# One list of 62 regular edges for each row in place of two lists of 32, in a sparse graph-attention kernel

## The chip, the core and the metric

The kernel runs on one core of one Trainium2 chip. The metric is device time in microseconds (us) for one execution. TensorE is called PE (its weight loads PEld), VectorE DVE, ScalarE ACT, GpSimd POOL, and SyncE SP.

## The reference

There are 3327 nodes with 128 features each, and a dense adjacency matrix in which about 64 entries of a row are not zero. Two layers follow each other: a four-head attention layer, in which only the nonzero entries of the row count, and a normalised graph convolution. Cut to what matters:

```python
def head(x, A, w1, w2, a, Wlin):              # x: layer-normed and relu'd features
    E = leaky_relu((x @ w1)[:, None, :] + (x @ w2)[None, :, :], 0.01)
    s = jnp.tanh(E @ a / 8.0) * 8.0
    s = jnp.exp(s) * A
    s = s / jnp.sum(s, axis=-1, keepdims=True)
    return leaky_relu(s @ x @ Wlin.T, 0.01)

x = x + concatenate([head(h, adj, ...) for 4 heads]) @ w
# layer 1: A_t = adj + I, D its row sums
x = x + relu(D^-1/2 A_t D^-1/2 @ (relu(layernorm(x)) @ W.T + b))
```

## The kernel before

The kernel treats the adjacency as lists of edges. The rows are padded to 3328, which makes 26 blocks of 128 rows, and each block is worked through in two halves of 64 rows (half-blocks, `hb`).

**Lists.** For each row, `prep` codes the columns of the nonzero entries (L401), takes the eight largest codes of each of 64 segments (L405), and draws from the left and the right half of the columns a sorted list of SLOTS = 32 edges each, eight at a time: a MAX8 (L434) gives eight, a MATCH_REPLACE (L436) strikes them out. These 64 edges are the row's regular slots. What is left over goes into up to EXTRA = 40 further entries (L457, L460), and those of 64 rows are packed into three tiles of extra edges (OVT = 3), addressed by the comparison matrix `oi`. If any edge did not fit, a flag would send the whole program down a dense path after the sparse one; this is not seen in the profile.

**Tiles.** A regular tile has 128 edges: 8 rows of the block by 16 slots. A half-block thus has 32 regular tiles in four windows `w` of WT = 8 tiles, and a fifth window (w = NW = 4) with the three extra tiles. The row numbers in tile order come from a product of the lists, spread by `modsel` (L440), with `tmask` (L447, L450: `idx`); `pex` brings each row's score term into tile order in the same way (L541).

**Gathers.** For each tile, POOL issues one indirect DMA (L562), which brings 128 table rows of up to 709 floats: 64 adjacency weights, 133 features and sums, and four heads of 128 projected features. The windows have four buffers `g`, the extra tiles one buffer `ge`.

**Stages.** Half a window, four tiles, is a stage m (m = 0 to 7 regular, m = 8 the extra tiles). `stage_z`: for each head PE transposes the four tiles into z (L587), and DVE takes the maximum with the negative own projection of the row, x1n (L599, into r); in m = 8 PE adds the own projection (L590) and ACT does the relu (L596). `stage_r`: PE reduces r with `sel` to scores s (L610). After each window, `finish` runs: ACT copies the scores (L618), DVE picks the adjacency weights of each edge out of the gathered rows (`wq`, L622, with `qmask`), PE turns the scores (L627), DVE adds two terms (sc, L630 and L633), ACT computes tanh and exp, DVE multiplies exp and weight into `wt` (L649), and PE adds everything up into `ag` with eight products (L658), each with 32 columns of weights: 4 heads by 8 rows. For the extra tiles, the weights `wo` cover all 64 rows (L665, L667), and ag takes six products of 128 columns (L676). `close` then finishes the half-block.

**Order.** The program's order on every engine is fixed when the kernel is built. The loop over stages calls `slot()` six times for each stage. At each slot the running `finish` and `close` generators take one step (up to their next `yield`), `advance` takes a share of the NPREP = 72 steps of the next preparation, and `fetch` issues what gathers have a buffer. At the start of a block the next block's preparation is half done, so that the coding and most list rounds of the next but one fall into the second half-block, and the index products, extra rounds and `oi` into the first. In program order, the finish of window 3 (stages 6 and 7) starts at the end of stage m = 8; its products into `wt` are issued at the start of the next half-block's stage m = 1, and its ag products at that stage's end; the finish of the extra tiles comes one stage later.

```python
            for i in range(-1, n + 1):
                if i + 1 < n:
                    slot()
                if 0 <= i < n:
                    ...
                    rs[i] = stage_z(blks[b], hb, m, slot)
                if 0 <= i - 1 < n:
                    ...
                    stage_r(blks[b], hb, m, rs.pop(i - 1))
                    if m % 2 or m == NG - 1:
                        ends.append(finish(blks[b], hb, m // 2))
                    slot()
```

Of the kernel before, what the change touches and what calls it, by code (L numbers as in the profile page):

```python
# [9 lines left out]
F32 = mybir.dt.float32  # L10
AF = mybir.ActivationFunctionType
OP = mybir.AluOpType
AX = mybir.AxisListType
# [46 lines left out]
SLOTS = 32  # L60
EXTRA = 40
# [3 lines left out]
COLS = 709  # L65
FEAT = 64
# [162 lines left out]
def _sparse_layers(tc, nc, x, adj, w1, w2, a, wlin, w, gw, gb, gb_sb, gwT, x_sb, dinv, flag, ident, out):  # L229
# [18 lines left out]
    NT = 32  # L248
    NG = 9
    WT = 8  # L250
    NW = NT // WT
    LATE = 1

    with ExitStack() as l0:
# [16 lines left out]
        tmask = res.tile([P, 16], F32, name="tmask")  # L271
        modsel = res.tile([P, P], F32, name="modsel")
        qmask = res.tile([P, 8], F32, name="qmask")
        hoff = res.tile([P, 2], F32, name="hoff")
        lower = res.tile([P, P], F32, name="lower")
        first = res.tile([P, 16], F32, name="first")
# [19 lines left out]
        nc.gpsimd.iota(first, [[0, 2], [16, 4], [0, 2]], base=0, channel_multiplier=0, allow_small_or_imprecise_dtypes=True)  # L296
# [7 lines left out]
        for down in (hoff, rowid):  # L304
            nc.vector.tensor_scalar(down, down, -1.0, float(NP), op0=OP.mult, op1=OP.add)

        nc.gpsimd.affine_select(tmask, ones[:, :16], [[-8, 16]], OP.is_ge, 0.0, base=0, channel_multiplier=1)
        nc.gpsimd.affine_select(tmask, tmask, [[8, 16]], OP.is_ge, 0.0, base=7, channel_multiplier=-1)

        nc.gpsimd.affine_select(qmask, ones[:, :8], [[-16, 8]], OP.is_ge, 0.0, base=0, channel_multiplier=1)  # L310
        nc.gpsimd.affine_select(qmask, qmask, [[16, 8]], OP.is_ge, 0.0, base=15, channel_multiplier=-1)
# [32 lines left out]
        def prep(b, k):  # L344
# [21 lines left out]
            def known_step(j0, js, at):  # L366
# [5 lines left out]
                if j0 == 0:  # L372
                    k.part1 = pb.tile([P, P], F32, name="part1")
                    nc.scalar.copy(k.part1, pq[:, :P])
                else:
                    nc.vector.tensor_add(k.part1, k.part1, pq[:, :P])
# [52 lines left out]
            lists = pb.tile([P, 64 + 46], F32, name="lists")  # L429
            k.lists = lists  # L430
            for c in range(2):
                for r in range(SLOTS // 8):
                    top = lists[:, SLOTS * c + 8 * r:SLOTS * c + 8 * r + 8]
                    nc.vector.max(top, cand[:, c, :SOME])  # L434
                    yield
                    nc.vector.match_replace(out=cand[:, c, :SOME], in_to_replace=top, in_values=cand[:, c, :SOME], imm_value=0.0)  # L436
                    yield

            lq = pb.tile([P, 4, 8, 16], F32, name="lq", bufs=1)
            nc.vector.tensor_tensor(lq, modsel.rearrange("p (q s) -> p q s", q=8)[:, None].to_broadcast([P, 4, 8, 16]),  # L440
                                    lists[:, :64].rearrange("p (c s) -> p c s", c=4)[:, :, None, :].to_broadcast([P, 4, 8, 16]), OP.mult)
            yield
# [3 lines left out]
            for c in range(4):  # L446
                nc.tensor.matmul(pm[:, 16 * c:16 * c + 16], lq[:, c].rearrange("p q s -> p (q s)"), tmask, start=True, stop=True)  # L447
            yield
            idx = pb.tile([P, NW, 16], mybir.dt.int32, name="idx")
            nc.vector.scalar_tensor_tensor(idx, pm[:, :64].rearrange("p (c t) -> p c t", c=4), -float(ROW),  # L450
                                           first[:, None, :].to_broadcast([P, NW, 16]), op0=OP.mult, op1=OP.add)
            k.idx = idx
            yield
            flat = cand[:, :, :SOME]
            for r in range(EXTRA // 8):
                top = lists[:, 64 + 8 * r:64 + 8 * r + 8]
                nc.vector.max(top, flat)  # L457
                yield
                if r < EXTRA // 8 - 1:
                    nc.vector.match_replace(out=flat, in_to_replace=top, in_values=flat, imm_value=0.0)  # L460
                yield
# [7 lines left out]
            ext = lists[:, 64:]  # L469
            some = pb.tile([P, EXTRA], F32, name="some")  # L470
            cnt = pb.tile([P, 1], F32, name="cnt")
            nc.vector.tensor_scalar(some, ext[:, :EXTRA], 0.0, None, op0=OP.is_gt, op1=OP.add, accum_out=cnt)
            nc.scalar.copy(ext[:, 41:42], rowid)
            nc.scalar.copy(ext[:, 42:42 + H], p_all[:, b, H:])
# [5 lines left out]
            nc.vector.tensor_sub(ext[:, 40:41], hoff[:, :1], pm[:, :1])  # L480
            end = pb.tile([P, 1], F32, name="end")
            nc.vector.tensor_sub(end, ext[:, 40:41], cnt)
# [3 lines left out]
            nc.vector.tensor_reduce(lsum, lists[:, :64 + EXTRA], AX.X, OP.add)  # L486
# [8 lines left out]
            nc.vector.tensor_scalar(oi, code[:, :2 * OVT * P], ext[:, 40:41], None, op0=OP.is_le)  # L495
# [7 lines left out]
            ex_ps = pm[:, :2 * OVT * 46].rearrange("p (t c) -> p t c", c=46)  # L503
# [3 lines left out]
            ex = pb.tile([P, 2 * OVT, 46], F32, name="ex")  # L507
# [3 lines left out]
            nc.vector.tensor_sub(rel, epos, ex[:, :, 40])  # L511
# [19 lines left out]
            for h in range(H):  # L531
# [3 lines left out]
            pmx = pb.tile([P, 16, H], F32, name="pmx")  # L535
            nc.vector.tensor_tensor(pmx, tmask[:, :, None].to_broadcast([P, 16, H]),
                                    p_all[:, b, None, :H].to_broadcast([P, 16, H]), OP.mult)
# [9 lines left out]
        def rows_in():  # L547
            state["turn"] += 1
            return pgs[state["turn"] % 4].tile([P, WT, ROW], F32, name="g")
# [246 lines left out]
        def allow(kind):  # L796
            state[kind] += 1
# [509 lines left out]
```

## Time and profile before

| | before |
|---|---|
| median of three runs | 2530.59 us (2528.16 to 2538.27) |
| the profiled execution | 2536.74 us, span 2534.9 us |
| busy share: PE, DVE, POOL, ACT | 90%, 80%, 71%, 28% |
| DMA | 838.58 MB, mean 331 GB/s |
| gathers | 1664 regular and 156 extra, mean 971 and 978 ns on POOL |
| first gather, first z, last regular gather | 67.1, 76.0, 2422.6 us |

The span is the time from the first instruction to the last in one profiled execution. A line of a group gives the source line, engine, operation, what is written and read, shapes and count; then the busy time in us, the mean of one instruction in ns, and the idle time of the engine just before these instructions with what ended it. Busy time counts overlapping instructions once, so it can be less than count times mean. A line of the timeline gives start, duration and, in brackets, the idle time before it. A line of the waits gives the total, the number and the longest of the waits of one line for another. PE's ends are modelled, so a busy PE is not PE at its peak.

### The profile page before, as it was taken

Reading aid. Unit: us, or ns where it says so; the run is one execution under the profiler, and the core shown is the slowest. Engines: PE = TensorE matmul, PEld = TensorE weight load, DVE = VectorE, ACT = ScalarE, POOL = GpSimd, SP = SyncE. Lnnn points to the kernel's source line nnn. Section 1 sums busy time; section 2 is a strip of 40 time slices with the busy share of each in tenths; the row PEclk is TensorE's granted clock in tenths of the full one; section 3 lists DMA queues with packets and bytes.
Section 4 is the critical chain, followed back from the end, with each engine's and each line's share of the span. In section 5 each row is a group of like instructions: output and inputs, shape, how many; then the busy total and the mean of one; then the engine's idle time right before and its main releaser. Section 6 shows DMA issues by size and latency. Waiting matters only on the chain.

```text
span 2534.9 us, 51974 instructions
## 1 busy us (share of the span) xinstructions
PE 2278.9 (90%) x19410; PEld 1586.2 (63%) x19410; DVE 2030.5 (80%) x6260; ACT 704.1 (28%) x1651; POOL 1791.8 (71%) x1873
## 2 busy tenths in 40 slices
PE   6689899988989998989998999999999899999898
PEld 4456666656666666666666666666666667675553
DVE  7678988888788888878888788988988888895433
ACT  4122233223223222322322322232232233222110
POOL 3577777777777777777777777777777777777620
PEclk9789999999999999999999999999999999999999
DMA  9999999999999999999999999999999999999995
GB/s 294 392 338 314 342 353 318 334 351 335 324 339 346 318 328 359 329 319 343 337 312 336 353 311 341 352 329 329 339 346 318 330 360 313 333 322 347 324 336 186
DMA packets 460759, 838.58 MB, mean 331 GB/s; under 512 B 209099, under 2 KB 318165, under 8 KB 457173
## 3 DMA queue, kind: packets, MB, share of 16 engines
q0 software_dynamic: 145600, 640.34, 71.0%
q1 hardware_dynamic: 219396, 140.96, 19.1%
q10 hardware_dynamic: 95504, 53.88, 7.0%
q8 instruction: 156, 2.56, 0.4%
q14 instruction: 103, 0.84, 0.1%
HBM read 765.93 MB, written 113.42 MB: 347 GB/s over the span
## 4 chain that ended last, share of the span: by engine, by line
PE 35%; DVE 24%; DMA 20%; POOL 11%; issue 7%; ACT 1%; SPq 0%; DVEq 0%; POOLq 0%; ACTq 0%
DMA g<-table,idx 13%; DVE r L599 11%; POOL g L562 10%; PE z L587 10%; PE s L610 6%; PE z L590 3%; DMA ge<-table,idxo 3%; PE z L937 2%; DVE cand L405 2%; PE tr L627 2%; PE ag L658 2%; DMA AT_d<-at 2%; PE tr L370 2%; PE tr L505 1%; DVE codes L401 1%
## 5 line engine op out<-in xcount | busy, mean ns | idle before, releaser
L562 POOL DMA_INDIRECT g<-table,idx x1664 | 1616.3, 971 | 568.3 <-issue 442.2
L599 DVE TENSOR_TENSOR r<-z,x1n 128x1024 f32<-128x1024 f32 x832 | 1010.1, 1215 | 65.5 <-PE z L587 63.9
L587 PE MATMUL z<-ident,g 128*128 128x128 f32 x6656 | 922.4, 278 | 151.9 <-DVE r L599 111.7
L587 PEld LDWEIGHTS z<-ident,g 128*128 128x128 f32 x6656 | 743.8, 142 | 366.9 <-DVE r L599 224.2
L610 PE MATMUL s<-r,sel 128*32 128x512 f32 (+1 forms) x3744 | 491.1, 597 | 0.7 <-ACT ssb L618 0.7
L618 ACT COPY ssb<-s 128x512 f32<-128x512 f32 x260 | 146.7, 564 | 524.6 <-PE s L610 522.5
L630 DVE TENSOR_TENSOR sc<-tr,g 128x32 f32<-128x32 f32 x208 | 38.5, 185 | 300.5 <-PE tr L627 300.5
L405 DVE MAX8 cand<-codes 128x8 f32<-128x52 uint16 x1664 | 215.3, 205 | 0.0
L562 POOL DMA_INDIRECT ge<-table,idxo x156 | 152.6, 978 | 47.5 <-issue 38.1
L638 ACT ACTIVATE th<-sc 128x32 f32<-128x32 f32 x260 | 58.3, 224 | 420.9 <-DVE sc L633 418.5
L590 PE MATMUL z<-oi,x1b 128*128 128x384 f32 x416 | 174.1, 501 | 0.0
L658 PEld LDWEIGHTS ag<-g,wt 128*32 128x32 f32 x3328 | 99.0, 110 | 115.3 <-issue 100.8
L357 ACT COPY at<-tr 128x512 f32<-128x512 f32 (+1 forms) x175 | 97.0, 554 | 222.2 <-PE tr L355 198.3
L627 PE MATMUL tr<-ident,ssb 128*128 128x128 f32 x988 | 153.1, 276 | 5.0 <-ACT ssb L618 4.5
L610 PEld LDWEIGHTS s<-r,sel 128*32 128x32 f32 x3744 | 73.9, 108 | 110.5 <-issue 86.4
L587 PEld LDWEIGHTS z<-ident,ge 128*128 128x128 f32 x624 | 81.4, 146 | 94.8 <-issue 28.5
L596 ACT ACTIVATE r<-z 128x768 f32<-128x768 f32 x104 | 84.3, 810 | 201.7 <-PE z L590 201.7
L658 PE MATMUL ag<-g,wt 128*32 128x133 f32 x3328 | 133.4, 278 | 0.0
L587 PE MATMUL z<-ident,ge 128*128 128x128 f32 x624 | 111.7, 283 | 21.1 <-DMA ge<-table,idxo 18.5
L627 PEld LDWEIGHTS tr<-ident,ssb 128*128 128x128 f32 x988 | 114.3, 141 | 15.3 <-ACT ssb L618 14.9
L355 PE MATMUL tr<-ident,adjb 128*128 128x128 f32 x676 | 107.4, 282 | 16.3 <-DMA adjb<-in_adj_dram 10.2
L401 DVE SCALAR_TENSOR_TENSOR codes<-adjb,code 128x832 uint16<-128x832 f32 x104 | 102.3, 1020 | 1.9 <-DMA adjb<-in_adj_dram 1.9
(188 smaller groups left out, 2350.4 us busy)
## 6 DMA issues: line engine op xcount, KB each, us to landing
adjb<-in_adj_dram SPq DMA_DIRECT2D x26, 1664.0 KB
table<-AT_d SPq DMA_DIRECT2D x52, 832.0 KB
AT_d<-at ACTq DMA_DIRECT2D x150, 256.0 KB
g<-table,idx POOLq DMA_INDIRECT x1664
table<-img SPq DMA_DIRECT2D x12, 1312.0 KB
adjb<-AT_d SPq DMA_DIRECT2D x18, 512.0 KB
g<-AT_d SPq DMA_DIRECT2D x7, 1024.0 KB
g<-AT_d ACTq DMA_DIRECT2D x5, 1024.0 KB
```

Of the source, the lines that this page charges most:

```text
L355: nc.tensor.transpose(pt[:, q, :], adjb[:, (j0 + q) * P:(j0 + q + 1) * P], ident)
L357: nc.scalar.copy(at[:, :n, :], pt[:, :n, :])
L401: nc.vector.scalar_tensor_tensor(codes[:, i], adjb[:, c0:c0 + part], 0.0, code[:, c0:c0 + part], op0=OP.not_equal, op1=OP.mult, accum_out= ...
L405: nc.vector.max(cand[:, c, 8:].rearrange("p (r s) -> p r s", s=32)[:, :, sgm % 32], codes.rearrange("p a b -> p (a b)")[:, sgm % 32 * SEG: ...
L562: return nc.gpsimd.indirect_dma_start(out=g[:, t, lo:COLS], out_offset=None, in_=tab, in_offset=bass.IndirectOffsetOnAxis(ap=at[:, t:t + 1 ...
L587: nc.tensor.matmul(z[:, i, q * P:(q + 1) * P], g[:, m % 2 * 4 + q, PROJ + h * D:PROJ + (h + 1) * D], ident, is_transpose=True, start=(q == ...
L590: nc.tensor.matmul(z[:, i, :n], k.x1b[:, h * D:(h + 1) * D], k.oi[:, hb * n:(hb + 1) * n], start=False, stop=True, skip_group_check=True)
L599: nc.vector.tensor_tensor(r.rearrange("p h (i s) -> p h i s", s=16), z.rearrange("p h (i s) -> p h i s", s=16), k.x1n[:, 2 * hp:2 * hp + 2 ...
L610: nc.tensor.matmul(k.s[32 * h:32 * h + 32, :n], sel[:, h, 31 - at:63 - at], rs[h // 2][:, h % 2, :n], start=(at == 0), stop=(at == 1 or m ...
L618: nc.scalar.copy(ssb[:, :nk * P], s[:, :nk * P])
L627: nc.tensor.transpose(pt[:, q, :], ssb[:, q * P:(q + 1) * P], ident)
L658: nc.tensor.matmul(ag[32 * cg:32 * cg + 32, u, :WORK], wt[:, t].rearrange("p h q -> p (h q)"), g[:, t, FEAT:FEAT + WORK], start=(w == 0 an ...
```

## The change

Each row now has one list of 62 regular edges, taken over all columns: two rounds of eight from either half, then further rounds over both halves together, which run on into the EXTRA = 42 entries of extra edges. The first 48 slots make three windows of eight tiles as before (8 rows by 16 slots). The last 14 slots make seven tiles in three shapes: four of 16 rows by 8 slots, two of 32 rows by 4 slots, one of 64 rows by 2 slots. The fourth window thus has LAST = 7 tiles, and a half-block 31 regular tiles and three of extra edges. Masks, index products, `pex`, r, `wq`, sc and the ag products follow the shapes; the last window's weights are written into `wo`, and its `wq` into the buffer of `am`, both shared with the extra tiles. A gathered row takes 712 places of its buffer in place of 720. NLIST and NPREP grow by two. `part1`, `pmx` and `some` have one buffer instead of two.

The core of the diff:

```diff
-SLOTS = 32
-EXTRA = 40
+SLOTS = 62
+EXTRA = 42
+WIDE = 712
...
+    LAST = WT - 1
+    SHAPE = ((8, 0, 16), (16, 16, 8), (32, 24, 4), (64, 28, 2))
+    EX = EXTRA + 6
...
-            for c in range(2):
-                for r in range(SLOTS // 8):
-                    top = lists[:, SLOTS * c + 8 * r:SLOTS * c + 8 * r + 8]
-                    nc.vector.max(top, cand[:, c, :SOME])
-                    yield
-                    nc.vector.match_replace(out=cand[:, c, :SOME], in_to_replace=top, in_values=cand[:, c, :SOME], imm_value=0.0)
-                    yield
+            both = cand[:, :, :SOME]
+            parts = [cand[:, c, :SOME] for c in range(2) for _ in range(2)] + [both] * ((SLOTS + EXTRA) // 8 - 4)
+            def lists_step(r):
+                top = lists[:, 8 * r:8 * r + 8]
+                nc.vector.max(top, parts[r])
+                yield
+                if r < len(parts) - 1:
+                    nc.vector.match_replace(out=parts[r], in_to_replace=top, in_values=parts[r], imm_value=0.0)
+                yield
+            for r in range(8):
+                yield from lists_step(r)
+            def by_tile(at, n, i):
+                rows = SHAPE[i][0]
+                slots = P // rows
+                big = [P, n, rows, slots]
+                nc.vector.tensor_tensor(lq[:, max(0, i - 1):max(0, i - 1) + n]..., OP.mult)
+            lq = pb.tile([P, 3, P], F32, name="lq", bufs=1)
+            by_tile(0, 3, 0)
...
+            lq = pb.tile([P, 3, P], F32, name="lq", bufs=1)
+            for i, at in ((1, 48), (2, 56), (3, 60)):
+                by_tile(at, 1, i)
...
+            for i, to in enumerate((pm[:, :16 * H], last[:, :, :4 * H], last[:, :, 4 * H:6 * H], last[:, :, 6 * H:])):
+                _, at, n = SHAPE[i]
+                nc.tensor.matmul(to, modsel[:, i], pmx[:, at:at + n].rearrange("p t h -> p (t h)"), start=True, stop=True)
...
         def stage_z(k, hb, m, slot):
-            n = 4 * P if m < 8 else OVT * P
+            n = 4 * P if m < LAST else OVT * P
...
+                    half = HALF * hb
+                    for lo, hi, slots, r0 in (((0, 2 * P, 4, half), (2 * P, 3 * P, 2, half)) if m == LAST else ((0, 4 * P, 8, half),)
+                                              if m == LAST - 1 else ((0, 4 * P, 16, half + 32 * (m % 2)),)):
+                        u = (hi - lo) // slots
+                        nc.vector.tensor_tensor(r[:, :, lo:hi]..., z[:, :, lo:hi]..., k.x1n[...], OP.max)
...
         def finish(k, hb, w):
+            if w == NW - 1:
+                wq = pb.tile([P, OVT, HALF], F32, name="am", bufs=1)
+                for i, (t, n) in enumerate(((0, 4), (4, 2), (6, 1))):
+                    ...
+                    nc.vector.tensor_tensor(wq[:, i]..., diag, qmask[...], OP.mult)
...
+            for at, m, n in ((0, 2, 4),) if nt == WT else ((0, 1, 4), (4, 1, 3)) if nt == LAST else ((0, 1, OVT),):
+                nc.vector.tensor_tensor(sc[:, at:at + m * n]..., pt..., g[...]..., OP.add)
...
+            if w == NW - 1:
+                wo = pv.tile([P, OVT, 8, H, 8], F32, name="wo")
+                for i, (t, n) in enumerate(((0, 4), (4, 2), (6, 1))):
+                    u = 8 // n
+                    for c in range(n):
+                        nc.vector.tensor_tensor(wo[:, i, u * c:u * c + u], pe[:, t + c, None, :, None].to_broadcast([P, u, H, 8]),
+                                                wq[:, i]..., OP.mult)
+                ...
+                for i, (t, n) in enumerate(((0, 4), (4, 2), (6, 1))):
+                    u = min(4, 8 // n)
+                    for c in range(8 // u):
+                        o = 32 * (u * c % 4)
+                        nc.tensor.matmul(ag[o:o + 32 * u, u * c // 4, :WORK], wo[:, i, u * c:u * c + u].rearrange("p g h q -> p (g h q)"),
+                                         g[:, t + (c if n > 1 else 0), FEAT:FEAT + WORK], start=False, stop=False, skip_group_check=True)
+                allow("g")
+                return
...
-        NLIST = 42
-        NPREP = 72
+        NLIST = 44
+        NPREP = 74
```

## The prediction

> **What bounds the kernel now.** I read the page first, for the engines and the costliest groups.
>
> ```profile
> PE 2278.9 (90%) x19410; PEld 1586.2 (63%) x19410; DVE 2030.5 (80%) x6260; ACT 704.1 (28%) x1651; POOL 1791.8 (71%) x1873
> L562 POOL DMA_INDIRECT g<-table,idx x1664 | 1616.3, 971 | 568.3 <-issue 442.2
> L599 DVE TENSOR_TENSOR r<-z,x1n 128x1024 f32<-128x1024 f32 x832 | 1010.1, 1215 | 65.5 <-PE z L587 63.9
> ```
>
> The 71% of POOL is deceptive: between gathers of 0.95 us lies an issue gap of 0.30 us (442.2 us in 1442 gaps), so a gather holds POOL for 1.25 us, and the 35 gathers of a half-block (64 rows) for 43.8 us. The queue is nearly full. So the next view is the time of one half-block: I take the first transpose into z (L587) of each half-block from the timeline and cut the windows there, four in a row.
>
> ```profile
> 1628.63:1672.89 44.26, 41.20 (x374) 29.41 (x370) 35.68 (x94) 11.49 (x33) 33.59 (x36) 1.00 0.99 317
> 1672.89:1716.73 43.84, 40.85 (x375) 29.43 (x371) 40.64 (x142) 14.83 (x31) 33.22 (x35) 1.00 1.00 354
> 1716.73:1760.99 44.26, 41.20 (x374) 29.41 (x371) 35.68 (x94) 11.49 (x33) 33.60 (x36) 1.00 0.97 311
> 1760.99:1805.48 44.49, 41.76 (x384) 30.38 (x380) 40.91 (x143) 14.71 (x31) 33.83 (x35) 1.00 1.00 358
> ```
>
> Columns: window, length, busy us of PE, PEld, DVE, ACT, POOL, clock, DMA share, GB/s. A first half-block (the first and third row) takes 44.26 us each time, with the same busy times to 0.01; of the 24 first half-blocks between 195 and 2298 us, 19 lie within 0.2 us of that. Data that arrived late would not repeat so. A second half-block takes 43.05 to 44.7 when nothing disturbs it. Next, who waits for whom between 200 and 2300 us:
>
> ```profile
> DVE sc L630 <- PE tr L627: 250.4, 80, 8.3
> PEld z L587 <- DVE r L599: 238.7, 239, 2.6
> PE z L587 <- DMA ge<-table,idxo: 17.9, 21, 2.4
> PE z L587 <- DMA g<-table,idx: 5.7, 12, 1.3
> POOL g L562 <- issue: 397.8, 1300, 1.6
> ```
>
> TensorE and VectorE wait for each other, hardly for data. So the half-block's length is a chain through PE and DVE, in fixed order, and the gathers run beside it at almost the same pace: they win only where the extra tile (ge) arrives late. Comparing stage lengths with their undisturbed values, I find such delays in 16 of the 47 half-blocks, 31.9 us in all. That is what fewer gathers can give back.
>
> Where the chain has room is seen in DVE's timeline:
>
> ```profile
> 1678.62 0.42 DVE L649 TENSOR_TENSOR wt<-pe,wq 128x256 f32<-128x256 f32 x1
> 1682.99 0.64 PE L658 MATMUL ag<-g,wt 128*32 128x133 f32 x16
> 1683.33 0.28 DVE L665 SCALAR_TENSOR_TENSOR am<-code,ex,ge 128x64 f32<-128x64 uint16 x1
> 1683.71 0.42 DVE L667 TENSOR_TENSOR wo<-pe,am 128x256 f32<-128x256 f32 x1
> ...
> 1714.75 0.30 DVE L434 MAX8 lists<-cand 128x8 f32<-128x136 f32 x1
> 1717.86 0.19 DVE L630 TENSOR_TENSOR sc<-tr,g 128x32 f32<-128x32 f32 x1 [2.42 <-PE tr L627]
> ```
>
> In the stage of extra tiles (m = 8) DVE idles: 2.42 us here, at the end of a second half-block, and 6.11 us at the end of a first one (1674.02). Elsewhere in a second half-block it is never free (40.6 busy + 2.4 = 43.0 of 43.84), so DVE work added there lengthens it one for one. In a first half-block it has about 2.5 us of other room.
>
> **Two rules of the Trainium skill.** "VectorE: DVE Perf Modes", section on the TRN2 errata, says that an fp32 tensor_tensor takes (N+151)/0.96 ns, a fixed part per instruction, so small pieces are dear. The trace agrees: N = 512 gives 691 (L440 shows 682), N = 256 gives 424 (L649: 416), N = 64 gives 224 (L622: 219). For 128 and 384 elements I interpolate the trace: 283 and 549. Not all of it is engine time: eight MAX8 with a mean of 205 ns take 1.01 us, so 0.08 of each overlaps its neighbour, and I charge duration less 0.08. "TensorEngine Tiling (Array Packing)", section Theoretical Speedup, says that weights of at most 32 columns run up to four at once, of at most 64 two, and wider ones alone. Again the trace agrees, and it has the price:
>
> ```profile
> L658 PE MATMUL ag<-g,wt 128*32 128x133 f32 x3328 | 133.4, 278 | 0.0
> L676 PE MATMUL ag<-ge,wo 128*128 128x133 f32 x624 | 79.4, 277 | 0.0
> L649 DVE TENSOR_TENSOR wt<-pe,wq 128x256 f32<-128x256 f32 x208 | 86.5, 416 | 0.0
> L434 DVE MAX8 lists<-cand 128x8 f32<-128x136 f32 x208 | 61.6, 296 | 1.3
> L436 DVE MATCH_REPLACE8 cand<-lists,cand 128x136 f32<-128x136 f32 x208 | 59.0, 284 | 0.0
> L457 DVE MAX8 lists<-cand 128x8 f32<-128x272 f32 x130 | 57.3, 441 | 2.7
> ```
>
> 133.4/3328 = 0.040 us for each 32-column instruction, 79.4/624 = 0.127 for each of 128 columns.
>
> **The change, part by part.** *Removed:* one of 35 gathers, 52 in all: 52 x 1.25 = 65 us of POOL, and 52 x 0.33 MB = 17 of 839 MB. Both lie beside the chain; worth only the 32 us of late data above. In stage m = 7 PE loses four transposes, and s (L610) in the next stage shrinks from 1.06 to 0.85 us (the 384-column form at 1675.23): -0.21, on the path, since PE is full in the ge stage. r of m = 7 becomes 512 + 256 elements: L914 690 and 425 for L599's 1215, less overlap -0.18, twice: -0.36.
>
> *Added in each finish of w = 3.* Seven multiplications into wo (four of 64, two of 128, one of 256 elements) for one wt: 4 x 0.14 + 2 x 0.20 + 0.345 - 0.335 = +0.97 us of DVE at the start of stage m = 1. One more sc: +0.09. Two more wq: +0.28, queued in the idle of the ge stage; free (0.28 each if that idle were gone). The eight ag matmuls keep their number (sixteen instructions) but become 64 and 128 columns wide: 8 x 0.064 (half of 0.127, as the page has it) + 8 x 0.127 = 1.53 for 0.64: +0.9 of PE. wo has one buffer, shared with the extra tiles' wo of the stage after (L667). So a **new wait**: the first L667 must wait until PE has read the old wo. In a second half-block ag ends at 1683.63 and L667 starts at 1683.71; with both engines some 1.1 us later from wo on and ag 0.9 longer, L667 waits about 0.9. Behind it on DVE stand the MAX8s, the part1 addition and the next r, for which PE's z waits. In a first half-block L667 comes 0.8 us after ag and nothing waits.
>
> *Added in each block's preparation.* Rounds 4 to 7 of the lists scan both halves: 441 for 296, and 427 (L460) for 284: +0.29 each. In a second half-block rounds 5 to 7 come in the idle after the last r (1713.16 to 1715.44): free; round 4 is on the path: +0.3. The index product becomes one of 384 and three of 128 elements for L440: 0.47 + 3 x 0.20 - 0.60 = +0.47, early in a first half-block. pex needs four products for one: six instructions more, 0.12 (as L447: 0.96 us for eight) or less than 0.2 (its weight load), about +0.6, on PE in the ge stage of a first half-block, where PE is full. Masks at the start stand in POOL's waits there (19 us for DVE neg); the first block's lists lie before the first gather, which waits 24.5 us for that preparation: +3 once with PE's extra round trip.
>
> *Sum for a block.* First half-block: wo 0.97 less the 0.51 that r (1722.38) waits for PE there, 0.47, 0.09, 0.6, -0.36, -0.21: **+1.05**. Second: 0.97 + 0.09 + 0.9 + 0.3 - 0.36 - 0.21: **+1.7**. With 24.5 such blocks (the last has nothing to prepare): 24.5 x 2.75 = +67; late data -32; start +3: **+38 us**. The profiled execution took 2536.7 us, so 2575; the median of the three runs lies 6.1 below it: **2569**.
>
> Bounds. Low: no wait for wo, its multiplications half covered, pex 0.3: about +1.3 for a block, the sum near zero, 2531. High: no overlap between small instructions (wo +1.41, index +0.72), the wait 1.5, all four rounds on the path: +5.6 for a block, +113, 2644. r with inner runs of 4 and 2 elements has no row; as no row here shows shape to matter (128x256 in runs of 8 takes 416), I take nothing for it, between 0 and +0.5 us a block, inside the high end.
>
> **Rivals.** *The gathers are the bound* (15%): POOL is without a pause, DMA shows shares of 0.97 to 1.00, and blocks fit POOL's pace; then 52 x 1.297 (the mean distance of two gathers) = 67 us go: 2463. Against it: the identical half-blocks, and lead: gathers land some 4 us before their first use. *The cover holds* (15%): DVE has 8.6 us of idle in a first half-block; with the steps of the preparation shifted by two in 74, the additions fall into it and the result is 2531 +- 15. Against it: most of that idle is in one place, the ge stage. *Worse than my bounds* (10%): the wait for the shared wo decides. From the point where ag of w = 3 ends over 2 us after the first L667 is ready, each half-block pays it: 52 x 2 = 104 in place of the 22 counted: 2651. *The change doesn't do what it says*: lists too short would send everything down the dense path. Counted on the inputs, the fullest half-block needs 362 of 384 extra edges, the fullest row 35 of 42; excluded.
>
> **The numbers.** My own case has 60%, mostly slower (56 of 60). Slower by over 0.5%: 0.56 + 0.10 + 0.03 = 0.69; within 0.5% (12.7 us, about what a measurement of this kernel can tell from no change): 0.14; faster 0.17. Own range 2531 to 2644; with the rivals, 2500 to 2635 leaves about 2 in 10 out.
>
> **What would show it.** Gathers x1612 + x156; PE's waits for ge gone; PE's waits for r (L599) longer; first half-blocks about 45.3, second about 45.5 us; DVE busy near 2127 (3.7 a block), the first wo of the extra tiles with an idle before it that PE's ag ends; POOL waiting for buffers (ag), which it hardly does now. Wrong, if half-blocks fall below 43.5 us with POOL still without waits, or if the wo products hide in the ge stage.

## The result and the profile after

The changed kernel takes 2563.9 us (median of five runs, 2562.45 to 2567.59), the kernel before, measured beside it, 2531.96 (2528.16 to 2538.27). The ratio is 1.0125, with a 95% interval of 1.0107 to 1.0143: slower by 32 us, where 38 were forecast. The profiled execution has a span of 2562.0 us, 27.1 longer than before. Of the three groups of experiments below, one was measured while the kernel before took its usual time, 2531.22 us, and the two others while it took 3238.38 and 3229.46 us, for a cause that is not settled, so that every experiment carries the time of the kernel before beside it, and times are compared only where that is the same.

The page of the kernel after, first its engines and then the groups of costly instructions that the prediction spoke of (`g` gathers, `r`, the extra tiles' `wo`, and PE's product into `tr`):

```profile
PE 2330.0 (91%) x19462; PEld 1650.9 (64%) x19462; DVE 2096.5 (82%) x6916; ACT 704.0 (27%) x1651; POOL 1791.6 (70%) x1839
...
L595 POOL DMA_INDIRECT g<-table,idx x1612 | 1612.2, 1000 | 596.7 <-issue 425.5
L636 DVE TENSOR_TENSOR r<-z,x1n 128x1024 f32<-128x1024 f32 (+1 forms) x936 | 984.6, 1064 | 51.5 <-PE z L620 51.4
...
L380 PE MATMUL tr<-at,x_sb 128*128 128x128 f32 x488 | 77.6, 303 | 60.0 <-DVE sc L677 56.7
...
L736 DVE TENSOR_TENSOR wo<-pe,am 128x256 f32<-128x256 f32 x156 | 66.4, 426 | 63.6 <-PE ag L712 59.9
```

There are 52 gathers fewer, and POOL is busy as long as before: a gather's mean went from 971 to 1000 ns. PE gained 51 us and DVE 66. The last two rows are waits: PE's L380 waits 56.7 us for DVE's sc (the kernel before: 20.8 for the same pair, L370 and L630), and L736 waits for ag, which is the new wait that was forecast. PE's waits for gathered data, which the chain could not hide before (ge 17.9 us), are not in the list of waits any more. PE's waits for r, which were forecast to grow, fell. From the lists of waits from 200 to 2320 us, two lines of before and then the line of after for r:

```profile
PE z L587 <- DVE r L599: 106.6, 149, 1.7
PE tr L370 <- DVE sc L630: 20.8, 22, 2.1
```

```profile
PE z L620 <- DVE r L636: 69.1, 106, 1.0
```

Cut at each half-block's first transpose into z, the +27.1 us divide like this. The start, up to the third half-block, is 1.6 us shorter. The 24 first half-blocks after it take 1071.5 us for 1062.9: +8.6, from a mean of 44.29 to one of 44.65. The 23 second half-blocks between them take 1070.8 for 1040.0: +30.7. What follows is 10.7 shorter. Of the 1040.0 us before, 29.5 were late data (stage m = 8 had a mean of 6.78 us, where 5.50 is its undisturbed length), so a second half-block without them took 1010.5/23 = 43.94, and now takes 46.55. These +2.6 have to be explained.

The windows of the kernel after show where they lie. Each half-block here is cut into stage m = 0, stage m = 1 and the rest; the first three rows are one second half-block, the last three the second half-block of the next block. Columns as in the prediction: length, busy us of PE, PEld, DVE, ACT, POOL, then the granted clock, DMA share and GB/s.

```profile
1231.17:1234.91 3.74, 3.19 (x33) 2.33 (x29) 2.57 (x7) 1.20 (x4) 2.83 (x4) 1.00 0.97 354
1234.91:1245.21 10.30, 7.72 (x67) 6.33 (x68) 8.94 (x37) 1.86 (x5) 8.17 (x8) 1.00 0.90 263
1245.21:1276.54 31.33, 29.40 (x266) 20.28 (x264) 30.87 (x110) 11.63 (x22) 23.43 (x25) 1.00 1.02 360
1321.21:1324.95 3.74, 3.19 (x32) 2.33 (x29) 2.57 (x7) 1.20 (x4) 2.83 (x4) 1.00 0.89 283
1324.95:1336.91 11.96, 9.38 (x68) 7.99 (x69) 9.00 (x37) 1.86 (x5) 8.21 (x8) 0.86 0.87 259
1336.91:1368.24 31.33, 29.39 (x267) 20.28 (x265) 30.85 (x110) 11.63 (x22) 22.18 (x24) 1.00 0.98 337
```

The first stage and the rest are equal to 0.01 us. Stage m = 1 is 1.66 us longer in the second case, and PE's granted clock in it is 0.86. PE's timeline of the two stages, full clock first, then the other:

```profile
1239.34 1.13 PE L380 MATMUL tr<-at,x_sb 128*128 128x128 f32 x8 [2.58 <-DVE sc L677]
1240.31 1.04 PE L620 MATMUL z<-ident,g 128*128 128x128 f32 x8
...
1329.38 1.86 PE L380 MATMUL tr<-at,x_sb 128*128 128x128 f32 x8 [2.58 <-DVE sc L677]
1331.03 1.91 PE L620 MATMUL z<-ident,g 128*128 128x128 f32 x8
```

Both wait the same 2.58 us for sc. After it the same eight instructions take 1.13 us in one and 1.86 in the other, the next eight 1.04 and 1.91. All 22 waits of this kind are 2.58 us long (56.7/22; the kernel before: a mean of 0.95, 18 of the 22 about 0.76). Taking the window of each second half-block, 10 of 23 have the full clock and a mean of 45.39 us, 13 have a clock of 0.96 and a mean of 47.45. The two groups are not alike otherwise: PE's instructions in stage m = 1 grow from 51 to 68 from the first block to the last, and with them the half-block at full clock, from 43.76 to 47.05 us, and the 13 are mostly late ones. Between neighbours the difference is 1.4 to 1.7 us. Length times the clock that is missing comes to 22.2 us over the 23 half-blocks, all of it in stage m = 1. In the kernel before it is 11.9, of which 3.4 in that stage.

What PE waits for is seen in DVE's timeline of the same stage (the kernel after):

```profile
1325.76 1.22 DVE L636 TENSOR_TENSOR r<-z,x1n 128x1024 f32<-128x1024 f32 x1
1326.89 0.55 DVE L415 MAX8 cand<-codes 128x8 f32<-128x52 uint16 x4
1327.35 1.35 DVE L700 TENSOR_TENSOR wo<-pe,am 128x64 f32<-128x64 f32 x7
1328.62 0.55 DVE L415 MAX8 cand<-codes 128x8 f32<-128x52 uint16 x4
1329.09 0.15 DVE L677 TENSOR_TENSOR sc<-tr,ge 128x12 f32<-128x12 f32 x1
```

The first sc of the extra tiles (L677) reads a `tr` buffer, and PE's next product into tr needs that buffer. The seven wo products stand in front of it. In the kernel before, one product of 0.42 us (L649, at 1678.62) stood there, and PE's timeline of that half-block has:

```profile
1680.18 1.13 PE L370 MATMUL tr<-at,x_sb 128*128 128x128 f32 x8 [0.76 <-DVE sc L630]
```

So the wait was 0.76 us there, and the eight instructions took the 1.13 us of the full clock.

### The profile page after: what moved, and what is told of

Read it like the earlier page. It is cut to its first block, busy times and chain, and to the rows that moved or that the text cites. A ratio compares the mean times of both kernels' runs of the same rounds, so it can differ in the third digit from the quotient of the medians.

```text
span 2562.0 us, 52712 instructions
## 1 busy us (share of the span) xinstructions
PE 2330.0 (91%) x19462; PEld 1650.9 (64%) x19462; DVE 2096.5 (82%) x6916; ACT 704.0 (27%) x1651; POOL 1791.6 (70%) x1839
## 4 chain that ended last, share of the span: by engine, by line
PE 44%; DVE 29%; DMA 14%; POOL 7%; issue 5%; ACT 1%; SPq 0%; DVEq 0%; ACTq 0%; POOLq 0%
PE z L620 12%; DVE r L636 12%; DMA g<-table,idx 8%; PE s L648 8%; POOL g L595 7%; PE z L623 4%; DVE cand L415 3%; PE ag L712 3%; PE tr L673 2%; PE tr L380 2%; DVE cand L450 2%; PE ag L727 2%; DVE codes L411 2%; DMA ge<-table,idxo 1%; DVE lists L447 1%
## 5 line engine op out<-in xcount | busy, mean ns | idle before, releaser
L636 DVE TENSOR_TENSOR r<-z,x1n 128x1024 f32<-128x1024 f32 (+1 forms) x936 | 984.6, 1064 | 51.5 <-PE z L620 51.4
L620 PE MATMUL z<-ident,g 128*128 128x128 f32 x6448 | 904.8, 279 | 93.0 <-DVE r L636 73.0
L620 PEld LDWEIGHTS z<-ident,g 128*128 128x128 f32 x6448 | 730.9, 143 | 283.6 <-DVE r L636 185.2
L648 PE MATMUL s<-r,sel 128*32 128x512 f32 (+1 forms) x3744 | 480.3, 585 | 0.7 <-ACT ssb L657 0.7
L677 DVE TENSOR_TENSOR sc<-tr,g 128x32 f32<-128x32 f32 x260 | 41.6, 177 | 242.8 <-PE tr L673 242.7
L415 DVE MAX8 cand<-codes 128x8 f32<-128x52 uint16 x1664 | 222.2, 202 | 0.0
L623 PE MATMUL z<-oi,x1b 128*128 128x384 f32 x416 | 168.7, 487 | 0.0
L447 DVE MAX8 lists<-cand 128x8 f32<-128x272 f32 (+1 forms) x338 | 133.5, 395 | 4.5
L380 PE MATMUL tr<-at,x_sb 128*128 128x128 f32 x488 | 77.6, 303 | 60.0 <-DVE sc L677 56.7
L365 PE MATMUL tr<-ident,adjb 128*128 128x128 f32 x676 | 111.8, 290 | 18.1 <-DMA adjb<-in_adj_dram 10.2
L727 PEld LDWEIGHTS ag<-g,wt 128*32 128x32 f32 x2496 | 74.0, 110 | 71.1 <-issue 62.4
L736 DVE TENSOR_TENSOR wo<-pe,am 128x256 f32<-128x256 f32 x156 | 66.4, 426 | 63.6 <-PE ag L712 59.9
## 6 DMA issues: line engine op xcount, KB each, us to landing
g<-AT_d ACTq DMA_DIRECT2D x5, 1024.0 KB, 10.2
```

Of the source, the lines that this page charges most:

```text
L365: nc.tensor.transpose(pt[:, q, :], adjb[:, (j0 + q) * P:(j0 + q + 1) * P], ident)
L380: nc.tensor.matmul(pq[:, :P], x_sb[:, j0 + q, :], at[:, q, :], start=(q == 0), stop=(q == js[-1]))
L415: nc.vector.max(cand[:, c, 8:].rearrange("p (r s) -> p r s", s=32)[:, :, sgm % 32], codes.rearrange("p a b -> p (a b)")[:, sgm % 32 * SEG: ...
L447: nc.vector.max(top, parts[r])
L620: nc.tensor.matmul(z[:, i, q * P:(q + 1) * P], g[:, m % 2 * 4 + q, PROJ + h * D:PROJ + (h + 1) * D], ident, is_transpose=True, start=(q == ...
L623: nc.tensor.matmul(z[:, i, :n], k.x1b[:, h * D:(h + 1) * D], k.oi[:, hb * n:(hb + 1) * n], start=False, stop=True, skip_group_check=True)
```

## The experiments

Two theories stood against each other. The first is the prediction's: the wait of the extra tiles' wo for ag (L736) and the added DVE work lengthen the second half-block. The second came from the traces: the seven products keep back sc, PE waits for it, and then runs at a lower clock.

"At 2531 us" and the like name the time of the kernel before that was measured beside a run; a ratio is to that time. "Lost clock" below is length times missing clock, summed over the stages m = 1 of the 23 second half-blocks.

**The wait for the shared wo taken away**, by three tiles wo0 to wo2 in place of one, so that only the last of three depends on the last products:

```diff
-                wo = pv.tile([P, OVT, 8, H, 8], F32, name="wo")
+                wo = [pv.tile([P, 8, H, 8], F32, name=f"wo{i}") for i in range(OVT)]
```

At 3238 us: 

> The kernel after, with the weights wo of the last window and of the extra tiles in three buffers of one third each (same space) in place of one. So the first wo of the extra tiles waits only for the first eight ag instructions. Wait theory (the shared wo costs the second half-block, 1.3 us there and 0.6 us in a first one in the trace of after): the DVE waits for PE's ag (59.9 us in all) fall below 10 us and the time falls by 15 to 40 us, to 2525 to 2550. Rival (that wait only stands in for another one, since PE is behind at that place anyway): the waits move to r on z and the time stays within 5 us of 2564.

At 2531 us: 

> The same kernel as e1_wo_split (wo in three buffers of a third), once more, since in that call the kernel before itself took 3238 us, with waits that the profile cannot name. Where the kernel before takes about 2532 us: wait theory 2525 to 2550 us, DVE's waits for PE's ag under 10 us; rival within 5 us of 2564.

Measured at 2531 us: 2555.75 us, ratio to the kernel before 1.0099 (1.0078 to 1.0121); the span is 7.2 us under that of the kernel after. From the list of waits, 200 to 2320 us, of the kernel after and then of this one (total, number, longest):

```profile
DVE wo L736 <- PE ag L712: 47.1, 46, 2.5
PE tr L380 <- DVE sc L677: 56.7, 22, 2.6
```

```profile
DVE wo L737 <- PE ag L712: 8.4, 21, 1.4
PE tr L380 <- DVE sc L677: 56.7, 22, 2.6
```

The forecast wait was real, and 38.7 us of it went, but only 7 of the time, which ends up between the ranges of theory and rival. First half-blocks fell from 44.65 to 44.38, 24 x 0.27 = 6.5 us. Second ones fell by 8.3 us in all, 3.4 of them because 11 and not 13 lost clock; so the wait cost about 0.2 us each. What follows the last of these half-blocks took 6.9 us more, which is not explained. PE's wait for sc stayed, and most of the lost clock (18.8 us). At 3238 us the ratio was 1.0251 (1.0219 to 1.0282); the lost clock was 10.2 us there.

**The seven products placed after sc.** The generator gives way three times before the products and two times after, in place of five times after, so ag stays where it was:

```diff
+                later = 3 if k.b < NB - 1 or hb == 0 else 0
+                for _ in range(later):
+                    yield
...
-                yield
-                yield
-                yield
-                yield
-                yield
+                for _ in range(5 - later):
+                    yield
```

At 3238 us: 

> The kernel after, with the seven wo products of the last window issued three slots later and the ag products at their old place (in the very last half-block as before). They then stand behind sc of the extra tiles and behind the first r of stage 1. Theory (the products delay sc, which frees the bank that PE's next product into tr needs: PE waits 2.57 us there in a second half-block, and r then waits 1.42 us for z): PE's waits of tr for sc fall from 56.7 us to about 21 as before the change, and the time falls by 10 to 30 us. Rival (only the 0.97 us of work counts, wherever it stands): time within 5 us of 2564, or longer by up to 15 because ag now waits for wo.

At 2531 us: 

> The same kernel as e2_wo_late (the seven wo products three slots later), once more for the same reason. Where the kernel before takes about 2532 us: theory 2534 to 2554 us with PE's waits of tr for sc at about 21 us; rival 2559 to 2579 us.

Measured at 2531 us: 2526.87 us (16 runs, 2521.14 to 2533.41), ratio 0.9978 (0.9967 to 0.9989) to the kernel before, and 37 us under the kernel after. That is less than even the theory expected. Its windows, a second half-block cut as above, then DVE's and PE's timelines of stage m = 1:

```profile
1661.75:1665.49 3.74, 3.19 (x32) 2.32 (x28) 2.57 (x7) 1.20 (x4) 2.83 (x4) 1.00 0.86 296
1665.49:1674.52 9.03, 7.73 (x68) 6.34 (x69) 8.86 (x37) 1.86 (x5) 7.20 (x7) 1.00 0.88 254
1674.52:1706.68 32.16, 30.28 (x274) 21.22 (x273) 31.18 (x112) 11.56 (x22) 22.62 (x24) 1.00 0.99 344
```

```profile
1668.35 0.15 DVE L677 TENSOR_TENSOR sc<-tr,ge 128x12 f32<-128x12 f32 x1
...
1670.21 1.36 DVE L703 TENSOR_TENSOR wo<-pe,am 128x64 f32<-128x64 f32 x7
```

```profile
1668.64 1.13 PE L380 MATMUL tr<-at,x_sb 128*128 128x128 f32 x8 [1.29 <-DVE sc L677]
```

DVE does the same work, but sc goes first. PE waits 1.29 us for it (28.5 in all, 22 times, longest 1.3; 21 were expected), and the clock is 1.00 in every one of the 23 second half-blocks: no lost clock. Their mean is 44.58. Against the kernel after this is 46.55 - 44.58 = 1.97 each, 45 us; first half-blocks lose 0.3 each, 7 us; 38 remain, as measured. Of the 45, the clock makes up about 22. PE's wait for sc is 28 us shorter (56.7 - 28.5), which is a few us more than the rest. The wait of L736 for ag is gone too, and in its place PE's weight loads for ag wait for the products, 40.1 us in all; a cost of that was not found. At 3238 us the ratio was 1.0134 (1.0097 to 1.017); there too the lost clock of stage m = 1 was 0.0 in this kernel, where the three other versions of the kernel after measured there had 10 to 22 us. But its time was no better there than that of the next experiment, which keeps the lost clock: the gain of 37 us is shown only at 2531 us.

**The steps of the preparation back to 72.** One yield is taken out after each index product:

```diff
-        NLIST = 44
-        NPREP = 74
+        NLIST = 42
+        NPREP = 72
```

> The kernel after, with the two added steps of the preparation taken out (one yield fewer after each index product), and NPREP 72, NLIST 42 as before the change, so that the preparation's steps fall on the slots of before. Theory (the shift put the coding, codes, in front of the first r of a second half-block, whose stage 0 takes 3.74 in place of 3.12 us): stage 0 back to 3.12 us and the time down by 10 to 20 us. Rival (DVE is busy throughout a second half-block, so order does not matter): within 5 us of 2564.

Measured at 3238 us: a ratio of 1.0127 (1.0095 to 1.016). In second half-blocks 22.2 us of clock were lost in stage m = 1, so the added steps are not what causes that. Stage m = 0 took 3.66 to 4.03 us and not the expected 3.12. That doesn't refute the theory, since two versions of the kernel before, at 3229 us, have 3.9 to 4.2 there; with the same 72 steps in the last experiment, at 2531 us, it is 3.12. The time cannot be judged without a run of the kernel after beside it.

**A 35th gather again**, of data that nothing uses, in a buffer place of the last window:

```diff
+            if n == LAST:
+                los.append(0)
+                queue.append((k, hb, w, lambda: nc.gpsimd.indirect_dma_start(out=g[:, LAST, :COLS], ...)))
```

At 3238 us: 

> The kernel after, with an eighth gather in each last window again (into the eighth tile of its buffer, which nothing reads): 35 gathers and the old DMA bytes for a half-block. Chain theory (PE and DVE set the length, gathers run beside): 0 to +15 us, 2564 to 2579. Rival (the saved gather is worth its full 1.25 us, and the additions ate it): +50 to +65 us, 2614 to 2629.

At 2531 us: 

> The same kernel as e4_gather35 (an eighth gather in each last window that nothing reads), once more for the same reason. Where the kernel before takes about 2532 us: chain theory 2564 to 2579 us; rival (a gather is worth its 1.25 us) 2614 to 2629 us.

Measured at 2531 us: 2578.74 us, ratio 1.0199 (1.0174 to 1.0223), 14.8 us over the kernel after. 52 gathers of 1.25 us would be 65 if the gathers set the pace. What came back is a wait for late data, from this kernel's list of waits:

```profile
PE z L624 <- DMA ge<-table,idxo: 7.8, 9, 1.3
```

Stage m = 8 of the second half-blocks grew from 5.26 to 5.74 us, 11 us in all. The gathers still run beside the chain, with the wait for the extra tile as the place where they show. At 3238 us the ratio was 1.0393 (1.0355 to 1.0432), 51 to 91 us above the three other versions of the kernel after; why a gather was dearer there stays open.

**34 gathers in the kernel before**, with ACT filling the last tile of window 3 instead:

```diff
+                if w == NW - 1:
+                    n = WT - 1
+                    nc.scalar.copy(g[:, n, 48:COLS], lower[:, :1].to_broadcast([P, COLS - 48]))
```

> The kernel before with 34 gathers for a half-block: the eighth gather of each last window is left out, and ACT fills its tile with a constant (0.75 us of ACT, which is 28% busy), so the sums of that tile are left out of the result. Nothing else of the change is in it. Chain theory (gathers run beside PE and DVE; only late data is won, 31.9 us between 195 and 2298 us, some 3 to 8 us at the start and some 10 at the end): 2482 to 2500 us, second half-blocks at 43.4 to 44.7 us without waits for ge. Rival (the gathers were the bound): 2466 us or less, first half-blocks below 44.0.

**Seven products in the kernel before**, `wt` of window 3 written in seven overlapping pieces, nothing else changed:

```diff
-                nc.vector.tensor_tensor(wt, pe[:, :, :, None].to_broadcast([P, WT, H, 8]),
-                                        wq[:, :, None, :].to_broadcast([P, WT, H, 8]), OP.mult)
+                for lo, n in ((0, 2), (2, 2), (4, 2), (6, 2), (0, 4), (4, 4), (0, 8)) if w == NW - 1 else ((0, 8),):
+                    nc.vector.tensor_tensor(wt[:, lo:lo + n], ...)
```

> The kernel before with one part of the change alone: in the last window, the product wt is made in seven instructions (four of 64, two of 128, one of 256 elements, some of it written twice) in place of one of 256. No new wait on a shared buffer, no wider ag. Order theory (these products stand in front of sc of the extra tiles, which frees the bank that PE's next product into tr needs, so that PE and then r wait): second half-blocks 1.5 to 2.2 us longer, first 0.4 to 1.0, the late data of 32 us mostly gone: 2545 to 2575 us. Rival (only their own time counts, 0.97 us, and half of it is covered): 2520 to 2540 us.

Both were measured at 3229 us: ratios of 0.9789 (0.9759 to 0.982) and 1.0015 (0.9968 to 1.0062). Neither time decides for the theory of its expectation. The first, as a ratio, lies just under the range of the chain theory (0.980 to 0.988), and it is 66 us less, 1.27 for each of the 52 gathers, as if they were the bound there; what fewer gathers alone would bring to the kernel before at 2531 us stays open. The second is no change that can be told, where the order theory expected a ratio of 1.005 to 1.017. What can be read is stage m = 1. From the lists of waits from 200 to 2320 us, first of 34 gathers (where sc stands in L633), then of seven products:

```profile
PE tr L370 <- DVE sc L633: 3.5, 3, 2.0
```

```profile
PE tr L370 <- DVE sc L630: 32.4, 15, 3.1
```

With one product the lost clock of stage m = 1 is 3.4 us, in 2 of 23 second half-blocks, as in the kernel before at its usual time. With seven it is 22.2, in 13 of 23, as in the kernel after. The products alone bring the lost clock about, without any of the other parts of the change. That they alone bring the longer time about is not shown: at 3229 us PE lost 207 us of clock in the 47 half-blocks of this run, and the 19 more of this stage are lost among them.

**ag with 32 columns only**, the weights of one row group for each product:

```diff
-                        o = 32 * (u * c % 4)
-                        nc.tensor.matmul(ag[o:o + 32 * u, ...], wo[:, i, u * c:u * c + u]...)
+                        e = (0, 4, 6)[i] + c
+                        o = 32 * (e % 4)
+                        nc.tensor.matmul(ag[o:o + 32, ...], wo[:, i, u * c]...)
```

> The kernel after, with the sixteen ag instructions of the last window given 32 columns of weights each, in the four column groups in turn, as in the windows before (the other rows' sums of those tiles are left out of the result). Their time should fall from 1.78 to 0.64 us. If PE's added time there is a cause of its own (stage 1 of a first half-block is full on PE, and the first wo of the extra tiles waits for it): 2535 to 2555 us. Rival (PE has room there, the products in front of sc decide): within 8 us of 2564.

Measured at 3229 us: a ratio of 0.9986 (0.9944 to 1.0028), with 15.4 us of lost clock. The sixteen instructions take 43.0 us in all, for 96.9 in the kernel after, but the time shows no difference that can be told from the kernel before, and no run of the kernel after stands beside it; so this says nothing about PE's added time.

**Late products, five in place of seven, and list rounds of 24 edges from either half** together:

```diff
-            parts = [... for _ in range(2)] + [both] * ((SLOTS + EXTRA) // 8 - 4)
+            parts = [... for _ in range(3)] + [both] * ((SLOTS + EXTRA) // 8 - 6)
...
+                    if n == 4:
+                        for j in range(u):
+                            nc.vector.tensor_tensor(wo[:, i, j::u], ...)
```

> The kernel of e2b_wo_late (2526.9 us) with two parts made cheaper: the four wo products of 64 elements become two of 128 (seven instructions to five, -0.16 us), and three rounds of the lists are drawn from either half in place of two (two rounds of 136 in place of 272 elements, up to -0.58 us for a block). DVE-bound theory for the second half-blocks: 0.3 to 0.7 us less for a block, 2510 to 2520 us. Rival (both lie in DVE's idle): 2524 to 2530 us.

Measured at 3229 us: a ratio of 1.0133 (1.0107 to 1.016). The lost clock of stage m = 1 is 0.0, as with late products alone; whether five products or the shorter rounds add to it is not settled, and the time cannot be judged against an expectation that holds for 2531 us.

**All three parts**: split wo, late products, 72 steps.

```diff
+                later = 3 if k.b < NB - 1 or hb == 0 else 0
+                for _ in range(later):
+                    yield
-                wo = pv.tile([P, OVT, 8, H, 8], F32, name="wo")
+                wo = [pv.tile([P, 8, H, 8], F32, name=f"wo{i}") for i in range(OVT)]
...
-        NPREP = 74
+        NPREP = 72
```

> The kernel after with all three mends: wo in three buffers, its seven products three slots later, and the preparation back at 72 steps. If the parts are separate causes that add up (each 10 to 30 us), the second half-blocks come back to about 44.5 us and the time is 2500 to 2525 us, less than the 2532 of the kernel before. Rival (DVE's and PE's added work is the cost, and order only moves it): 2550 us or more.

Measured at 2531 us: 2590.34 us, ratio 1.024 (1.0219 to 1.0262): the slowest at 2531 us. The parts do not add up. Second half-blocks come back as expected (mean 44.40, no lost clock). First half-blocks went from 44.65 to 47.87, and 22.2 us of clock are lost there, where all other kernels at 2531 us lose nothing. This kernel's list of waits from 200 to 2320 us, and then the windows of stages m = 2 and 3 of a first half-block:

```profile
PE z L618 <- DVE r L634: 114.7, 151, 2.1
...
PE tr L471 <- DVE lq L461: 20.9, 23, 0.9
```

```profile
1215.33:1220.28 4.95, 2.95 (x27) 1.81 (x25) 4.61 (x13) 0.58 (x1) 3.73 (x5) 1.00 0.99 355
1220.28:1226.63 6.35, 6.35 (x41) 5.34 (x41) 5.03 (x14) 0.83 (x4) 4.79 (x6) 0.73 0.89 280
```

PE comes to the index product's transposes before DVE has made `lq`. That belongs to the two yields taken out: over the whole run, PE waits 25.1 us for it here and 13.4 with 72 steps alone, and at most 4.3 in the split wo, the late products and the kernel after. Further on PE idles 2 us of stage m = 2 (2.95 of 4.95 busy) for r. In the next stage it is never idle but has 0.73 of its clock. It looks like the same pattern in another place, a wait and then a lower clock; which of the three parts brings how much of the 3.2 us is not shown.

## Why the prediction was right, and where its sum was not

**What bounds the kernel** was read rightly. The half-block is a chain through PE and DVE in fixed order. A gather more for each half-block costs 14.8 us and not 65, so in the kernel after the gathers are not the bound, and the late products, also with one gather fewer for each half-block, are only 4 us faster than the kernel before: the rival with 2463 us is out. At 3229 and 3238 us a gather counted for 1.27 us and more, and what sets the pace there is not settled. One sign of the chain came out the other way: PE's waits for r fell, from 106.6 to 69.1 us, while its waits for sc rose.

**Late data, -32.** PE's waits for gathered tiles between 200 and 2320 us are gone. Of the 31.9 us, 29.5 had lain in second half-blocks. The sum holds, its reason only in part: put back into the longer chain, the 35th gather costs 14.8 us and not 32. So over half of the 32 us is won without saving a gather, in half-blocks that are longer; that these leave the gathers more time is likely, and not tested.

**First half-block, +1.05: mis-sized**, it was +0.36. Stages 0, 1 and 8 grew by 0.57, 0.84 and 0.46 us, 1.87 in all. The last, pex less the smaller s, had been put at 0.6 - 0.21 = 0.39. Stages 2 to 7 gave 1.5 of this back. I had let the work find cover only once, in the 0.51 us of r; the chain had more.

**Second half-block, +1.7: close without the lost clock, in part by luck, and a term was missing.** Without its lost clock (22.2/23 = 0.97 us) it takes 45.59, and before, without late data and lost clock of stage m = 1, 43.94 - 0.15 = 43.79: +1.80. But the parts of the sum were others. Of the 0.9 us for the wait for wo, only about 0.2 were there; and the seven products, charged with 0.97, made PE's wait for sc 1.63 us longer. On top come 22.2 - 3.4 = 19 us of lost clock, for which there was no term. The step that failed is the cost of "seven multiplications into wo": I charged their 0.97 us as DVE time and asked only who waits for wo. I did not ask who is queued behind them on DVE, and the answer was sc, which frees the buffer that PE's next product needs. A wait of 0.76 us stood at that place in the trace of before.

**The new wait for wo.** It came: 32.6 us in 22 second half-blocks, 1.5 each, where 0.9 was forecast, and 14.5 in the 24 first ones, 0.6 each, where none was. Its cost was wrong: with wo split, the second gained about 0.2 us each and the first 0.27. The rival in which this wait decides (2651) is out.

**Sizes of single instructions.** The DVE prices hold: 216, 280 and 413 ns for wo of 64, 128 and 256 elements (219, 283 and 426 were used), 549 for the index product of 384. The sixteen ag instructions take 1.78 us, not 1.53 (see the end). DVE busy rose by 66 us, not 96. The start, put at +3, came out 1.6 shorter, and the end 10.7 shorter; these I had not worked out. So the forecast of +38 came near the measured +32 (27.1 between the two profiled spans) by luck in part: the terms that were too high (first half-blocks, by 24 x 0.7 = 17 us, start and end, by 15) stood against 23 x (2.6 - 1.7) = 21 us missing in second half-blocks, most of it lost clock. The high bound has a slip: its own terms, 24.5 x 5.6 - 32 + 3, give 108 and not 113; nothing rests on it.

## What to carry to other kernels

When work is added to one engine, price its position and not only its length: name the next instruction behind it on that engine, and who waits for it. A wait of PE can cost more than its length, because what follows may run at a lower clock: here a wait of 2.58 us was followed 13 times of 22 by a loss of 1.7. So read the granted clock of the stage beside every new wait. In this kernel the order of the same instructions was worth 37 us, and 52 gathers 14.8.

## What the hardware showed

PE's clock after a short wait was not expected. In the kernel after, after equal waits of 2.58 us, it fell in 13 cases of 22; in the kernel with late products, after waits of 1.29 us, in none of 22. What sets the 13 apart is where the wait falls. In all 14 traces the granted clock is either 1.00 or 0.50, and it changes only on a grid of 3.413 us, to within 5 ns, which is the same from the start of a run to its end. The windows of the kernel after are cut on that grid here, each time a stretch with most of a wait of 2.58 us in it and then the next: 1.92 us of the first wait lie in its stretch, and all of the second wait.

```profile
1237.43:1240.84 3.41, 1.50 (x13) 1.53 (x14) 3.38 (x18) 0.69 (x3) 2.69 (x3) 1.00 1.01 273
1240.84:1244.25 3.41, 3.41 (x33) 2.23 (x32) 2.42 (x11) 0.58 (x1) 2.61 (x3) 1.00 0.90 290
1326.18:1329.59 3.41, 0.83 (x8) 0.62 (x7) 3.38 (x20) 0.70 (x2) 2.73 (x3) 1.00 0.79 204
1329.59:1333.00 3.41, 3.41 (x18) 3.41 (x18) 1.92 (x9) 0.57 (x3) 2.57 (x3) 0.50 0.98 317
```

The whole next stretch runs at half the clock, which loses 3.41/2 = 1.71 us, and 13 x 1.71 = 22.2. In the kernels before and after, the split wo, the 35th gather and the late products, PE waits for sc in front of these products 110 times. In the 38 cases where 2.00 us or more of the wait lie in one stretch, the next has half the clock; in the 72 with at most 1.95 us, none has. So a wait of 1.29 us was safe wherever it fell, and one of 2.58 was hit or spared by its place on the grid. This is shown for this wait with little other idle time around it, and not as a rule for every wait: at 3229 and 3238 us waits of 1.7 us were followed by half the clock too. The Trainium skill, "TensorE: Matmul & The Clock Gate", section "HAM oscillation — how this bites in real kernels", says that gaps of more than about 3.4 us let the clock fall to half. The half agrees; here 2.58 us were enough in more than half of the cases, so the measurement decides.

The sixteen ag instructions of the last window also took 0.25 us more than estimated, but not because two products of 64 columns fail to run at once. In the trace of the kernel after, they start in pairs, 0.007 us apart, and the pairs follow each other after 0.107 to 0.16 us; the products of 128 columns start 0.113 us apart, as in the trace of before. What is added stands where the width changes: two distances of 0.207 and 0.218 us there, in place of 0.113. Why the change costs that is not shown.
